# A graph network kernel: ACT's relu into a tile of its own, and six gather buffers in place of eight

## The chip, the cores and the metric

The kernel runs on one core of a Trainium2 chip. The time is the device time of one execution in microseconds (us); several executions are taken and their median is compared. The engines are PE (TensorE, matmuls; its weight loads are shown as PEld), DVE (VectorE), ACT (ScalarE), POOL (GpSimd) and SP (SyncE). Each works through its own instructions in their order and waits for the others by semaphores.

## What is computed

A graph has 6250 nodes with 128 features each and 100000 edges, sorted by their target node `dst`; targets are dense at the low node numbers. There are two GINE layers, which also read a row for each edge, and then two GIN layers, which don't. Cut to the sums over edges, and with the layer norms and the residual additions named only:

```
h = relu(layernorm(x))
for l in 0, 1:                                   # GINE
    msg = relu(h[src] + edge_attr)               # one row of 128 numbers for each edge
    agg = segment_sum(msg, dst)
    h = relu(relu(batchnorm((h + agg) @ W1[l] + b1[l])) @ W2[l] + b2[l])
x = x + h
h = relu(layernorm(x))
for l in 0, 1:                                   # GIN
    agg = segment_sum(h[src], dst)
    h = relu(((1 + eps) * h + agg) @ wa.T + ba) @ wb.T + bb
x = x + h                                        # the relu of GIN comes after its first layer only
```

## The kernel before

**Groups.** The edges are cut into 98 groups of 1024 (128 partitions x G = 8 edges; the last group is smaller). For each group of a GINE layer (the loop at L958) the program issues, in this order:

1. `load_rows` (L620): SP loads the group's edge rows, 512 KB, three groups ahead (`AHEAD`).
2. `gather` (L635): POOL issues eight indirect DMAs (L639), one for each of the 8 edges of a partition. Each brings 128 rows of 512 bytes from the node table in DRAM to the tile `g`, 128 x 1024 float32, 4 KB in each partition. `g` has eight buffers in the GINE layers and four in the GIN layers. A gather into a buffer waits until the last reader of the group that used it before is done.
3. `places` (L644): DVE makes the one-hot matrix `onehot` of the edges' target columns (L648), as wide as the group's span of nodes.
4. `Counter.count` (L734): beside the sums, the two GINE layers count how many edges lead from each node to each window of target nodes, which the GIN layers use for the first 70 groups' edges (their sums are then dense products, L1051). One or two units of 256 edges are counted in an iteration: DVE makes one-hots `lo_j` and `at_j` (L741, L744), PE multiplies them (L756) into a PSUM bank `pa`, and DVE adds the bank to the window `win` (L732, in `flush`), one unit later. ACT clears windows (L718) and SP stores them.
5. `sums` (L652): DVE adds the edge rows to `g` in place (L655), ACT applies relu to `g` in place (L656), PE multiplies `g` by `onehot` in 8 float32 terms (L660; 16 matmul instructions) into a PSUM bank `pe`. PE uses `g` as its weights.
6. `Columns.later` and `add` (L690 to L697): DVE adds `pe` of the group before this one (`BEHIND` = 1) to the columns of `acc` (L692).

Within an iteration, then, DVE has the order: one-hots, count one-hots and window additions, L655 of group s, L692 of group s-1. PE has the counts' matmuls and then L660 of group s. ACT has clears and then L656. The order is written out by hand for all five engines (`in_order`, L220); only semaphores delay an instruction.

Between the layers the nodes' own work runs in chunks of 512 nodes (`Steps`): batch norm and two products, and a table of the new features is written to DRAM, which the next layer's gathers read. In the second GINE layer, the first layer's own terms are made again chunk by chunk inside the loop (L972 to L977; ACT L842, PE L331, ACT L853). The GIN layers (loop at L1134) gather for the last 28 groups only, rows of 768 bytes (bf16 in three parts), and call `sums` without edge rows: there `g` goes to PE as gathered.

`general` (L1155) is a slow path for inputs whose targets are spread in another way. It isn't taken with these inputs.

Of the kernel before, what the change touches and what calls it, by code (L numbers as in the profile page):

```python
# [9 lines left out]
F32 = mybir.dt.float32  # L10
# [3 lines left out]
AF = mybir.ActivationFunctionType  # L14
# [3 lines left out]
P = 128  # L18
D = 128
# [3 lines left out]
G = 8  # L23

W = 152
# [3 lines left out]
BEHIND = 1  # L29
# [64 lines left out]
def gnn_kernel(ctx: ExitStack, tc: tile.TileContext, t: dict, out: bass.AP):  # L94
# [21 lines left out]
    nc = tc.nc  # L116
# [10 lines left out]
    NG = NGF + 1  # L127
# [32 lines left out]
    edge = gine_pools.enter_context(tc.tile_pool(name="edge", bufs=1))  # L160
# [3 lines left out]
    srcs = big.tile([P, NG * G], I32)  # L164
# [230 lines left out]
    for b in range(0, CODES, P):  # L395
        n = min(P, CODES + CODES % 2 - b)
# [238 lines left out]
    def gather(pool, table, n, idx, bufs):  # L635
        width, kind = (3 * D, BF16) if in_parts(table) else (D, F32)
        g = pool.tile([P, G, width], kind, name="g", bufs=bufs)
        for j in range(G):
            nc.gpsimd.indirect_dma_start(  # L639
                out=g[:n, j, :], out_offset=None, in_=table,  # L640
                in_offset=bass.IndirectOffsetOnAxis(ap=idx[:n, j : j + 1], axis=0))
        return g

    def places(pool, table, dl, w):  # L644

        onehot = pool.tile([P, G, W], BF16 if in_parts(table) else F32, name="onehot",
                           bufs=3)[:, :, :w]
        nc.vector.tensor_tensor(onehot, cols[:, None, :w].to_broadcast([P, G, w]),  # L648
                                dl[:, :, None].to_broadcast([P, G, w]), ALU.is_equal)
        return onehot  # L650

    def sums(g, n, onehot, rows):  # L652

        if rows is not None:
            nc.vector.tensor_add(g[:n], g[:n], rows[:n])  # L655
            nc.scalar.activation(g[:n], g[:n], AF.Relu)  # L656
        pe = bank_e()[:, : onehot.shape[-1]]
        terms = [(j, f) for j in range(G) for f in range(0, g.shape[-1], D)]
        for j, f in terms:
            nc.tensor.matmul(pe, g[:n, j, f : f + D], onehot[:n, j, :], start=(j, f) == terms[0],  # L660
                             stop=(j, f) == terms[-1])
        return pe
# [289 lines left out]
    for l in range(2):  # L952

        first_stages, end = batch_norm(l)
        steps, rest = Steps(first_stages), list(chunks())
        cs = Columns(brow)
        u, first_u, last_u = (0, 0, half) if l == 0 else (half, half, NU)
        for s in range(NG):  # L958
            n = P if s < NGF else RP
            for r in range(l * NG + s, min(l * NG + s + AHEAD + 1, 2 * NG)):  # L960
                if r not in rows:
                    rows[r] = load_rows(gine, r % NG, P if r % NG < NGF else RP, AHEAD + 2)
            g = gather(edge, tables[l], n, srcs[:, s * G : (s + 1) * G], 8)
            onehot = places(edge, tables[l], dloc[:, s, :], plan.group(s))
            while u < last_u and (cost[u] - cost[first_u]) * (NG - 6) < (s + 1) * (
                    cost[last_u] - cost[first_u]):
                counter.count(u)
                u += 1
                if u == NU:
                    counter.end()  # L970
            counter.some_chores()
            if own_later:  # L972

                got = None
                for stage in own_stages:
                    got = stage(*own_later[0], got)
                own_later.pop(0)  # L977
            cs.ready(max(s - BEHIND, 0))
            cs.later(s, sums(g, n, onehot, rows.pop(l * NG + s)), BEHIND)
            rows[l * NG + s] = None  # L980
            steps.step()
            ready = gine_ends[rest[0][2] + rest[0][3]]
            if ready is not None and ready <= s + 1 - BEHIND:
                steps.begin(rest.pop(0))
            if l == 0 and s == AHEAD:
                unplanned = nc.values_load(total[0:1, 0:1], min_val=0, max_val=1)
        if l:
            ahead[:] = chunks()
            load_ahead(x)
        while cs.late:  # L990
            cs.add(*cs.late.pop(0))
        for chunk in rest:
            steps.begin(chunk)
            steps.step()
        steps.end()
        if l == 0:
            own_stages = gine_nodes(0, *end())[:3]
            staged(*gine_rows(tables[1], own_stages[0]))
            own_later = list(chunks())
# [96 lines left out]
    for l in range(2):  # L1096
        stages = gin_nodes(l)
        if l == 0:
            def high_part(c, b0, n0, w, z):
                pt, xp = rows_of(bank_n, z, w), xps[1]  # L1100
                h = work.tile([P, CB, D], F32, name="h")
                for n, b in parts_of(w):
                    to = xp[:n, b0 + b.start : b0 + b.stop, :D]
                    nc.scalar.copy(to, pt[:n, b, :])
                    nc.vector.tensor_tensor(h[:n, b, :], pt[:n, b, :], to, ALU.subtract)
                return h

            stages = (*stages, high_part, parts_stages(xps[1], tables[3])[1])
        made, steps, rest, cs = products[l], Steps(stages), list(chunks()), Columns(brow)

        def pieces_to(n):
            while made.done < min(n, len(order)):
                made.piece()
                for _ in range(5):
                    if own_later:
                        _, b0, n0, w = own_later.pop(0)
                        of_parts(xps[0], b0, -(-w // P), own["eps1"], acc[:, n0 : n0 + w])

        def begin_nodes(s):


            u = made.counted()
            for chunk in rest:
                counted, gathered = (d[chunk[2] + chunk[3]] for d in (counted_ends, gine_ends))
                by_counts = counted is not None and u >= counted
                by_groups = gathered is not None and s >= gathered and (
                    u == NU or chunk[2] >= gathered_from)
                if by_counts or by_groups:
                    rest.remove(chunk)
                    steps.begin(chunk)  # L1130
                    return

        start = made.done
        for s in range(KG, NG):  # L1134
            n = P if s < NGF else RP
            g = gather(gin, tables[2 + l], n, srcs[:, s * G : (s + 1) * G], 4)
            onehot = places(gin, tables[2 + l], dloc[:, s, :], plan.group(s))
            pieces_to(start + max(3, -(-(s - KG + 1) * (len(order) - start) // (NG - KG - 1))))
            cs.ready(max(s - BEHIND, KG))
            cs.later(s, sums(g, n, onehot, None), BEHIND)  # L1140
            steps.step()
            begin_nodes(s + 1 - BEHIND)
        while cs.late:
            cs.add(*cs.late.pop(0))
        if l == 0:
            made.load()
        for chunk in rest:
            steps.begin(chunk)
            steps.step()
        steps.end()  # L1150
# [39 lines left out]
    def of_windows(pool, table, g, n, with_rows):  # L1190

        col = g * G
        idx = small.tile([P, G], I32, name="idx")
        dl = small.tile([P, G], F32, name="dl")
        if isinstance(g, int):
            nc.vector.tensor_copy(idx, srcs[:, col : col + G])
            nc.vector.tensor_scalar_add(dl, dloc[:, g, :], float(W))
            at_g = slice(g, g + 1)
        else:
            nc.vector.tensor_copy(idx, srcs[:, bass.ds(col, G)])  # L1200
            nc.vector.tensor_scalar_add(
                dl, dloc.rearrange("p g j -> p (g j)")[:, bass.ds(col, G)], float(W))
            at_g = bass.ds(g, 1)
        k = nc.values_load(wrow[0:1, at_g], min_val=1, max_val=NW)
        b = nc.values_load(brow[0:1, at_g], engines=[mybir.EngineType.DVE],
                           min_val=0, max_val=N)
        with tc.For_i(0, k) as i:
            nc.vector.tensor_scalar_add(dl, dl, -float(W))
            g_t = gather(pool, table, n, idx, 2)
            rows = load_rows(pool, g, n, 2) if with_rows else None  # L1210
            pe = sums(g_t, n, places(pool, table, dl, W), rows)
            at_c = nc.s_assert_within(b + i * W, min_val=0, max_val=N)
            a = acc[:, bass.ds(at_c, W)]
            nc.vector.tensor_add(a, a, pe)
# [29 lines left out]
```

## Time and profile before

| what | value |
|---|---|
| median of 10 runs | 3326.07 us (3320.42 to 3335.35) |
| the profiled execution, its own time | 3324.98 us |
| its span, first to last instruction | 3322.9 us |
| mean granted clock of TensorE | 0.73 |
| busy: PE, PEld, DVE, ACT, POOL | 1820.7, 1138.4, 1376.6, 454.8, 2039.5 us |
| gathers L639: count, mean | 2016, 985 ns |
| adds L655: count, mean | 196, 1219 ns |
| relus L656: count, mean | 196, 1056 ns |
| gathers of GINE layer 0: first start, last end | 41.5 us, 1217.0 us |
| gathers of GINE layer 1: first start, last end | 1276.7 us, 2412.5 us |
| gathers of the GIN layers | 2542.6 to 3276.2 us |

How to read the lines of the profile: `L639 POOL DMA_INDIRECT g<-table,srcs x2016 | 1986.7, 985 | 1086.7` means line 639 of the kernel, engine, operation, what it writes and reads, how many; then the busy time in us, the mean of one in ns, and the idle time of that engine just before these instructions, with what ended it. "issue" stands for no wait that the profile could tell, "remote" for a semaphore whose source it couldn't name. Lines of the time line begin with the start and the duration in us; the bracket at the end is the idle time before, and what ended it. PE's starts are recorded, its ends are modelled.

### The profile page before, as it was taken

The numbers are of one execution on the slowest core, as the hardware profiler recorded it, in microseconds if no ns is written. First come the engines' busy times: TensorE is split into PE (matmuls) and PEld (weight loads), VectorE is DVE, ScalarE is ACT, GpSimd is POOL, SyncE is SP. The second block draws the span as 40 slices with busy tenths as digits, with TensorE's granted clock in tenths as the row PEclk, the third lists the DMA queues.
The fourth block names the chain that finished last, engine by engine and source line by source line (L and its number), as shares of the span: only waits on it lengthen the run. The fifth ranks groups of instructions, "written<-read, shape, count | busy, mean of one in ns | idle before, by whom it ended". The sixth has DMA issues, their size and how long they took to land. (4 is left out here: it accounts for less than half of the span.)

```text
span 3322.9 us, 27768 instructions
## 1 busy us (share of the span) xinstructions
PE 1820.7 (55%) x8459; PEld 1138.4 (34%) x8460; DVE 1376.6 (41%) x3051; ACT 454.8 (14%) x579; POOL 2039.5 (61%) x2118
## 2 busy tenths in 40 slices
PE   1355445544444453355543454344557678858997
PEld 0233333333323342243432333222333334424443
DVE  5355455455555552244554455355552111111112
ACT  1200001010111112121110111111032001110000
POOL 6466666666676646666666666666614566546662
PEclk9999995556666676555555556666678888878998
DMA  3323242424243424233424344243447455545663
GB/s 117 113 89 91 89 127 89 129 88 130 86 134 95 124 84 135 69 96 121 135 90 121 93 133 133 85 128 100 151 119 231 147 171 169 184 136 185 222 218 122
DMA packets 259227, 421.87 MB, mean 127 GB/s; under 512 B 40864, under 2 KB 187088, under 8 KB 259068
## 3 DMA queue, kind: packets, MB, share of 16 engines
q1 hardware_dynamic: 173532, 184.05, 17.9%
q0 software_dynamic: 71424, 146.03, 14.7%
q10 hardware_dynamic: 14112, 89.92, 7.6%
q8 instruction: 69, 1.13, 0.1%
q14 instruction: 90, 0.74, 0.1%
HBM read 352.48 MB, written 67.36 MB: 126 GB/s over the span
## 5 line engine op out<-in xcount | busy, mean ns | idle before, releaser
L639 POOL DMA_INDIRECT g<-table,srcs x2016 | 1986.7, 985 | 1086.7 <-issue 900.4
L660 PE MATMUL pe<-onehot,g 128*128 128x16 f32 (+25 forms) x4480 | 745.4, 334 | 583.5 <-issue 241.8
L660 PEld LDWEIGHTS pe<-onehot,g 128*128 128x128 f32 x3136 | 610.1, 293 | 647.0 <-ACT g L656 301.8
L756 PE MATMUL pa<-at_j,lo_j 128*128 128x450 f16 (+22 forms) x1172 | 422.5, 498 | 649.3 <-DVE win L732 345.3
L1051 PE MATMUL pa<-piece,xp 128*128 128x512 f16 x2058 | 498.0, 395 | 66.5 <-issue 64.2
L732 DVE TENSOR_TENSOR win<-win,pa 128x450 f32 (+17 forms) x586 | 315.5, 575 | 408.8 <-remote 304.4
L756 PEld LDWEIGHTS <-lo_j 128*128 128x128 f16 x1172 | 157.7, 140 | 857.5 <-issue 466.1
L656 ACT ACTIVATE g<-g 128x1024 f32<-128x1024 f32 x196 | 207.0, 1056 | 1545.0 <-DVE g L655 817.3
L692 DVE TENSOR_TENSOR acc<-acc,pe 128x112 f32 (+18 forms) x252 | 61.1, 243 | 778.8 <-remote 328.3
L744 DVE TENSOR_SCALAR at_j<-numbers,code 128x1470 f16<-128x1470 f16 (+13 forms) x560 | 363.0, 648 | 0.0
L1051 PEld LDWEIGHTS <-xp 128*128 128x128 bf16 x2058 | 204.5, 100 | 352.2 <-issue 146.5
L655 DVE TENSOR_TENSOR g<-g,rows 128x1024 f32<-128x1024 f32 x196 | 238.8, 1219 | 23.9 <-DMA g<-table,srcs 20.1
L648 DVE TENSOR_TENSOR onehot<-numbers,dloc 128x896 bf16<-128x896 f32 (+23 forms) x252 | 224.4, 891 | 4.6 <-issue 4.6
L741 DVE TENSOR_SCALAR lo_j<-numbers,slo 128x128 f16<-128x128 f16 x560 | 153.5, 274 | 0.0
L660 PEld LDWEIGHTS <-g 128*128 128x128 bf16 (+1 forms) x1344 | 90.4, 105 | 78.7 <-issue 55.0
L801 DVE BATCH_NORM_STATS2 bst<-pn 128x6 f32<-128x512 f32 (+1 forms) x26 | 17.3, 666 | 213.7 <-remote 153.0
L718 ACT COPY win<-zero 128x1001 f32<-128x1001 f32 x98 | 92.9, 1019 | 74.3 <-remote 74.3
L692 DVE TENSOR_TENSOR acc<-acc,pa 128x256 f32 x28 | 11.8, 421 | 182.9 <-remote 116.7
L920 ACT ACTIVATE y<-pn,vcols 128x512 f32<-128x512 f32 (+1 forms) x26 | 17.1, 659 | 472.3 <-PE pn L331 421.2
L319 POOL TENSOR_SCALAR h<-xs,rs 128x128 f32<-128x128 f32 x49 | 21.4, 452 | 91.1 <-DVE rs L312 85.5
L828 DVE TENSOR_TENSOR xs<-xs,pn 128x512 f32<-128x512 f32 (+1 forms) x26 | 17.0, 654 | 78.9 <-PE pn L347 51.0
L802 ACT COPY acc<-pn 128x512 f32<-128x512 f32 (+1 forms) x26 | 14.6, 560 | 247.2 <-DVE bst L801 201.6
(162 smaller groups left out, 637.0 us busy)
## 6 DMA issues: line engine op xcount, KB each, us to landing
rows<-in_edge_attr SPq DMA_DIRECT2D x194, 512.0 KB
piece<-counts ACTq DMA_DIRECT2D x98, 896.0 KB
counts<-win SPq DMA_DIRECT2D x98, 448.0 KB
g<-table,srcs POOLq DMA_INDIRECT x2016
table<-xp SPq DMA_DIRECT2D x24, 384.0 KB
x_first<-in_x SPq DMA_DIRECT2D x8, 384.0 KB
table<-x_first SPq DMA_DIRECT2D x8, 384.0 KB
xs<-table SPq DMA_DIRECT2D x12, 256.0 KB
```

The costliest lines, as they stand in the source:

```text
L639: nc.gpsimd.indirect_dma_start(out=g[:n, j, :], out_offset=None, in_=table, in_offset=bass.IndirectOffsetOnAxis(ap=idx[:n, j : j + 1], axi ...
L648: nc.vector.tensor_tensor(onehot, cols[:, None, :w].to_broadcast([P, G, w]), dl[:, :, None].to_broadcast([P, G, w]), ALU.is_equal)
L655: nc.vector.tensor_add(g[:n], g[:n], rows[:n])
L656: nc.scalar.activation(g[:n], g[:n], AF.Relu)
L660: nc.tensor.matmul(pe, g[:n, j, f : f + D], onehot[:n, j, :], start=(j, f) == terms[0], stop=(j, f) == terms[-1])
L692: nc.vector.tensor_add(a, a, sums)
L718: self.chores.append(lambda v=flat[:, q * n : (q + 1) * n], n=n: nc.scalar.copy(v, self.zero.to_broadcast([P, n])))
L732: nc.vector.tensor_add(v, v, pa[:, : n * w].rearrange("p (b w) -> p b w", w=w))
L741: nc.vector.tensor_scalar(lo_j, cols16[:, MID : MID + P], slo[:, col : col + 1], None, op0=ALU.is_equal)
L744: nc.vector.tensor_scalar(at_j[:, :width], cols16[:, :width], code[:, col : col + 1], None, op0=ALU.is_equal)
L756: nc.tensor.matmul(pa[:, : n * w], los[j], ats[j][:, b * w : (b + n) * w], start=j == 0, stop=j == UT - 1)
L1051: nc.tensor.matmul(pa, xp[:, q * QB + b, i * D : (i + 1) * D], v[:, :, b, :], start=q + b + i == 0, stop=q == NQ - 1 and b == QB - 1 and i ...
```

## The change

`sums` takes one more argument, the pool. Where there are edge rows, it allocates a tile `m` of the same shape as `g`, with two buffers, ACT writes its relu into `m`, and PE's matmuls read `m`. The GINE loop's `gather` is called with six buffers. The calls for places without edge rows only pass a pool, and no `m` is made there.

```diff
-    def sums(g, n, onehot, rows):
+    def sums(g, n, onehot, rows, pool):
 
         if rows is not None:
             nc.vector.tensor_add(g[:n], g[:n], rows[:n])
-            nc.scalar.activation(g[:n], g[:n], AF.Relu)
+            m = pool.tile([P, G, D], F32, name="m", bufs=2)
+            nc.scalar.activation(m[:n], g[:n], AF.Relu)
+            g = m
         pe = bank_e()[:, : onehot.shape[-1]]
...
-            g = gather(edge, tables[l], n, srcs[:, s * G : (s + 1) * G], 8)
+            g = gather(edge, tables[l], n, srcs[:, s * G : (s + 1) * G], 6)
...
-            cs.later(s, sums(g, n, onehot, rows.pop(l * NG + s)), BEHIND)
+            cs.later(s, sums(g, n, onehot, rows.pop(l * NG + s), edge), BEHIND)
...
-            cs.later(s, sums(g, n, onehot, None), BEHIND)
+            cs.later(s, sums(g, n, onehot, None, gin), BEHIND)
...
-            pe = sums(g_t, n, places(pool, table, dl, W), rows)
+            pe = sums(g_t, n, places(pool, table, dl, W), rows, pool)
```

## The prediction

> **What bounds the kernel now.** I read the page first, then the waits, then the time line of each engine. The change touches the two layers with edge rows (GINE), 159.9 to 1217.0 and 1276.7 to 2412.5 us of the span. The page gives two of the steps in question:
>
> ```profile
> L639 POOL DMA_INDIRECT g<-table,srcs x2016 | 1986.7, 985 | 1086.7 <-issue 900.4
> ...
> L656 ACT ACTIVATE g<-g 128x1024 f32<-128x1024 f32 x196 | 207.0, 1056 | 1545.0 <-DVE g L655 817.3
> ```
>
> A group is eight gathers. They follow each other at 0.95 + 0.30 us, so a group takes POOL at least 10.0 us, and in layer 1 some 10.35 us, since a few gathers take 1.2 to 2.0 us. The adds L655, counted in the time line, come every 11.7 us in both layers. POOL alone doesn't explain 11.7, and DVE (busy 1376.6 us of the span) and ACT (454.8) even less. The list of waits names the rest:
>
> ```profile
> DVE acc L692 <- remote: 445.0, 33, 59.4
> ...
> DVE win L732 <- remote: 304.4, 38, 18.7
> ```
>
> DVE sits idle some 750 us before two instructions that read a result of PE in PSUM. What PE does then is plainest where its work is simple, at the start of the third layer. PE's time line, then POOL's:
>
> ```profile
> 2517.19 27.36 PE L1051 MATMUL pa<-piece,xp 128*128 128x512 f16 x126
> ...
> 2573.84 0.27 PE L790 MATMUL pe<-ident_b,xp 128*128 128x128 bf16 x1 [3.23 <-issue]
> 2575.94 0.27 PE L790 MATMUL pe<-ident_b,xp 128*128 128x128 bf16 x1 [1.83 <-issue]
> ...
> 2589.73 4.00 PE L790 MATMUL pe<-ident_b,xp 128*128 128x128 bf16 x36 [1.18 <-ACT acc L792]
> ```
>
> ```profile
> 2542.61 1.01 POOL L639 DMA_INDIRECT g<-table,srcs  x1 [17.56 <-DMA piece<-counts]
> ...
> 2581.53 0.95 POOL L639 DMA_INDIRECT g<-table,srcs  x1 [0.30 <-issue]
> ```
>
> While POOL rests, 126 matmuls take 27.36 us. POOL then gathers without a break from 2542.6 to 2582.5; some 15 us into that, PE falls to one small matmul every 1.4 to 3.5 us, and it recovers at 2585 to 2588, some 3 to 5 us after the last gather. One coincidence proves nothing, so here is an ordinary cycle of layer 0, from the time lines of POOL, of DVE and of ACT:
>
> ```profile
> 464.56 0.94 POOL L639 DMA_INDIRECT g<-table,srcs  x1 [0.30 <-issue]
> 468.82 0.94 POOL L639 DMA_INDIRECT g<-table,srcs  x1 [3.32 <-issue]
> ```
>
> ```profile
> 468.18 0.83 DVE L732 TENSOR_TENSOR win<-win,pa 128x300 f32 x2 [9.70 <-remote]
> ```
>
> ```profile
> 470.57 1.06 ACT L656 ACTIVATE g<-g 128x1024 f32<-128x1024 f32 x1 [14.76 <-DVE g L655]
> ```
>
> POOL gathers from 445.13 to 465.50, finds no free buffer and stops; 2.7 us later DVE, stuck for 9.70 us, gets PE's result, and 0.64 us after that POOL goes on. ACT's relu of the next group comes only later. And one of layer 1, in the same three views:
>
> ```profile
> 1816.43 0.95 POOL L639 DMA_INDIRECT g<-table,srcs  x1 [0.30 <-issue]
> 1822.00 0.95 POOL L639 DMA_INDIRECT g<-table,srcs  x1 [4.62 <-issue]
> ```
>
> ```profile
> 1821.30 0.22 DVE L692 TENSOR_TENSOR acc<-acc,pe 128x64 f32 x1 [16.00 <-remote]
> ```
>
> ```profile
> 1826.82 1.06 ACT L656 ACTIVATE g<-g 128x1024 f32<-128x1024 f32 x1 [20.38 <-DVE g L655]
> ```
>
> The stops are strikingly alike. Between groups, the time line of L639 has 39 of over 1 us in layer 0 after group 10 (128 us in all, mean 3.3) and 29 in layer 1 after its first run (123 us, mean 4.25), nearly all of 2 to 6 us. If PE's slow spells ended on their own, POOL would meet them at any phase and the stops would scatter widely. I read it so: **a long run of gathers holds PE's results back, and only POOL's stop lets them through.** POOL's time (10.0 to 10.35 us a group) plus its stops sets the 11.7. What carries the message inside the chip, no view here shows.
>
> The Trainium skill, "TensorE: Matmul & The Clock Gate", section "Seeing it yourself", has another cause for a slow PE: the clock gate, which it says has been seen stuck at a quarter for over 50 us, in events that aren't reliable. The row decides against it as far as the records go:
>
> ```profile
> 457.00:468.00 11.00, 3.99 (x18) 3.21 (x19) 1.48 (x5) 0.00 (x0) 6.62 (x7) 1.00 0.24 78
> ```
>
> Its granted clock is 1.00 in just the 11 us in which DVE waited. By that page the change would cost nothing (3326 us); by the row it costs the sum below.
>
> **The change, part by part.** *ACT's relu into m.* Same instruction, same 1.056 us; the nearest ACT row with two different tiles, L718, takes 1.019 us for 1001 elements, 1.042 scaled to 1024. Taken as nothing; bounds -0.01 and 0 us a group. *A wait on m.* It has two buffers, so relu of group s needs PE to be done with s-2. DVE's add of s stands behind L692 of s-2, which waits for just that, so ACT finds it done: 0. Were that cover gone, it would cost up to one group of matmuls (3.65 us) before relu, and win's clears L718 behind it. *PE's waits.* PE no longer waits for the gathers' landings, since it reads m; they had landed long before, and PE starts 0.05 us after relu's end (448.27 to 448.32): 0 to -10 us in all. *Memory.* Six buffers of g and two of m are what eight of g were. *Places without rows* (the GIN layers) make the same instructions as before.
>
> *The release of g.* Before, gather k waits for PE's matmuls of group k-8. After, it waits for ACT's relu of k-6. It is no matter of data coming late: the last gather of layer 1 ends at 2412.5 and its add comes at 2443.70; two groups less of lead (2 x 10.35 us) still leave 10 us. It is a matter of how long POOL stops. PE's result comes as before, about 3 us after the stop, but POOL then needs the add and the relu, too:
> - Layer 0: relu ends at 471.63, plus the 0.64 us to wake POOL, 472.27 in place of 468.82, so 3.45 us later; the cycle before (relu 447.21 + 1.06 + 0.63 against 445.13) gives 3.77. I take 3.6.
> - Layer 1: 1826.82 + 1.06 + 0.70 = 1828.58 in place of 1822.00: 6.6 us later, since DVE still has one-hots, counts and the add to do.
>
> In those extra microseconds POOL is quiet, PE runs freely and the consumers get ahead, so the next run of gathers is longer and there are fewer stops. Adds come 7.5 us apart in the fast stretches of layer 0 (445.91 to 453.45) and about 5.5 us apart in layer 1. Layer 0: 88 groups and 39 stops, 2.26 groups a stop. The next add needs a result that was held back at about 13 us after POOL's resumption; 3.6 us more let it through, so one more group: 3.26, 27 stops of 3.3 + 3.6 = 6.9 us, 186 in place of 128: **+58**. Layer 1: 89 groups, 29 stops, 3.07 a stop; 6.6/5.5 gives 1.2 more: 4.27, 20.8 stops of 10.85 us, 225 in place of 123: **+102**. Bounds: with no longer runs, 39 x 3.6 + 29 x 6.6 = +331; with two more groups a run, 20.7 x 6.9 - 128 = +15 and 17.6 x 10.85 - 123 = +68, together +83. I take the middle way because the gain in groups follows from the rows' own distances.
>
> At the start of layer 1 POOL gathers nine groups in one run (to 1368.2) while PE crawls; gather 106 then waits for a relu that came at 1380, so the run ends a group earlier: -10 us (bounds -10 and 0). Sum: 58 + 102 - 10 = **+150** on the span of 3322.9, 3473; the run lasts 2.1 us longer than its span, and the median 1.1 more than this run: **3476 us**.
>
> The Trainium skill, "Perfetto Trace Analysis", section "Identifying Performance Opportunities" (Optimization Strategy), says that a bubble which repeats on the engine that should be full can mean too few buffers. The stops above are such bubbles; as an estimate by that rule, 251 us x 8/6 would add 84 us, some 3410. It speaks against the change too, but doesn't see which event ends the bubble.
>
> **The rivals.** *Nothing moves.* PE's slow spells have a cause of their own (the float32 matmuls, the clock) and the gathers, landed dozens of us early, hide everything. For it: data are never late, and PEclk is 0.5 to 0.6 over most of layer 1. Against it: the slow spell at clock 1.00, and stops that are all alike. 3326 us; chance 0.17. *Faster: stops like those of GIN.* There POOL stops every group, near 2.2 us (3064.50 to 3067.69), and PE isn't starved. If in layer 0 the block comes one group earlier, before the results are held back, and ACT's message frees POOL without a crawl, each stop could shrink to 2.2 us: 39 x 1.1 + 29 x 2.05 = 102 less, 3224. It decides as soon as runs become shorter than some 13 us. Against it: consumers at 7.5 us a group outrun POOL at 10, so that POOL isn't blocked in time and the runs grow. Chance 0.13. *The change doesn't do what it says*: m keeps ACT waiting for PE after all, so that g hangs on PE with a lead of six: about 39 x 3.3 more stops' worth at worst, 3450. The order on DVE excludes it nearly: 0.02.
>
> **How the numbers follow.** Forecast 0.68, own range 3322.9 + 83 - 10 to 3322.9 + 331, with 3 us around it: 3399 to 3657. The measurement of this kernel tells about 0.2% (6.7 us) from no change. Slower: 0.68, the last rival, and 0.02 of the first: 0.72. Same: 0.13. Faster: 0.13 and the remaining 0.02 of the first: 0.15. The range must hold 0.8, so it takes in the first rival at its foot, and loses a little at the top: 3315 to 3620.
>
> **What would show it.** L656 becomes m<-g, still 1.06 us. POOL's stops in the GINE layers: about 27 and 21 in place of 39 and 29, some 7 and 11 us long, each ended by ACT's relu; runs of 3 and 4 to 5 groups. The adds come every 12.4 and 12.9 us. GIN keeps its length. It is wrong if the stops keep 3 to 4 us, or if DVE's long waits for PE go on after POOL has stopped; then PE is slow by itself.

## The result, and the profile after

| | before | after |
|---|---|---|
| median | 3324.46 us (31 runs) | 3497.41 us (9 runs, 3474.62 to 3513.14) |
| ratio | 1 | 1.0517, 95% interval 1.0500 to 1.0535 |
| span of the profiled execution | 3322.9 us | 3502.4 us |
| gathers of layer 0, first start to last end | 1175.5 us | 1286.5 us |
| gathers of layer 1 | 1135.9 us | 1220.8 us |

The change makes the kernel 5.2% slower. Two lines of `sums` are new, so the numbers move: the add is now L656, the relu L658, PE's matmuls L663, and `acc`, `win` and the counts L695, L735 and L759. The groups of the page for the gathers and the relu, with busy time, mean of one in ns, and idle time ahead of them:

```profile
L639 POOL DMA_INDIRECT g<-table,srcs x2016 | 1961.7, 973 | 1308.7 <-issue 625.9
...
L658 ACT ACTIVATE m<-g 128x1024 f32<-128x1024 f32 x196 | 207.0, 1056 | 1749.7 <-DVE g L656 786.6
```

The relu is the same 1056 ns, and the gathers are even a little shorter (973 in place of 985 ns). What grew is POOL's idle time, 1086.7 to 1308.7 us. The waits of the changed kernel (total us, times, longest) say whom POOL waits for:

```profile
DVE acc L695 <- remote: 625.8, 39, 60.3
...
POOL g L639 <- ACT m L658: 498.1, 60, 41.7
...
DVE win L735 <- remote: 376.8, 60, 20.1
```

Before, no such line of POOL's stood in the list; now 60 stops, 498.1 us, end with ACT's relu. DVE's two long waits for PE have grown with them, 445.0 to 625.8 us and 304.4 to 376.8 us. An ordinary cycle of layer 0, in the time lines of POOL, DVE and ACT (start, duration, and in brackets the idle time before and what ended it):

```profile
500.60 0.94 POOL L639 DMA_INDIRECT g<-table,srcs  x1 [0.30 <-issue]
508.07 0.94 POOL L639 DMA_INDIRECT g<-table,srcs  x1 [6.54 <-ACT m L658]
```

```profile
504.63 0.83 DVE L735 TENSOR_TENSOR win<-win,pa 128x300 f32 x2 [12.66 <-remote]
505.37 1.22 DVE L656 TENSOR_TENSOR g<-g,rows 128x1024 f32<-128x1024 f32 x1
```

```profile
506.75 1.06 ACT L658 ACTIVATE m<-g 128x1024 f32<-128x1024 f32 x1 [17.38 <-DVE g L656]
```

POOL stops at 501.54. PE's result reaches DVE at 504.63, 3.1 us after that, as it did before. Then, however, POOL waits on for the add (505.37), the relu (506.75 to 507.81) and 0.26 us more. In every stop over 1 us from group 6 on, the first gather now starts 0.3 us after the end of a relu; before, none of the stops of the steady part (from group 10 of layer 0, and all of layer 1) did; there POOL goes on within 1 us of a read by DVE that had waited for PE in 49 of 68.

The gaps over 1 us between POOL's groups, counted in the time line of L639, account for the time:

| stops | before | after | difference |
|---|---|---|---|
| layer 0, groups 1 to 9 | 2, 38.0 us | 3, 58.8 us | +20.8 |
| layer 0 from group 10 | 39, 127.9 us (mean 3.28) | 34, 236.0 us (mean 6.94) | +108.1 |
| layer 1 | 29, 123.2 us (mean 4.25) | 26, 216.8 us (mean 8.34) | +93.6 |

That is 222.5 us. The gathers' own busy time in the two layers gives back 24.0 (1560.8 to 1536.8), the small gaps between gathers 2.6, the stretch between the layers' gathers 11.6 (59.7 to 48.1) and the one after them 4.8 (910.4 to 905.6): with a lead of two groups less, fewer adds are outstanding when the last gather ends. The rest is 179.5 us, the difference of the spans.

### The profile page after: what moved, and what is told of

Its sections match the earlier page's. It is cut to its first block, busy times and chain, and to the rows that moved or that the text cites. A ratio compares the mean times of both kernels' runs of the same rounds, so it can differ in the third digit from the quotient of the medians.

```text
span 3502.4 us, 27611 instructions
## 1 busy us (share of the span) xinstructions
PE 1808.9 (52%) x8459; PEld 1130.2 (32%) x8460; DVE 1379.1 (39%) x3051; ACT 455.2 (13%) x579; POOL 2014.2 (58%) x2118
## 4 chain that ended last, share of the span: by engine, by line
another core or an unknown queue 31%; PE 24%; issue 16%; DVE 14%; POOL 7%; ACT 4%; DMA 3%; DVEq 2%; ACTq 1%; SPq 0%; POOLq 0%
PE pa L1054 11%; PE pe L663 8%; POOL g L639 6%; DVE at_j L747 4%; DVE win L735 3%; DVE g L656 2%; PE pa L759 2%; ACT m L658 2%; DMA g<-table,srcs 2%; DVE lo_j L744 2%; PE pn L331 1%; DVE onehot L648 1%; ACT win L721 1%; DVE acc L695 1%
## 5 line engine op out<-in xcount | busy, mean ns | idle before, releaser
L639 POOL DMA_INDIRECT g<-table,srcs x2016 | 1961.7, 973 | 1308.7 <-issue 625.9
L663 PE MATMUL pe<-onehot,m 128*128 128x24 f32 (+18 forms) x3136 | 635.5, 375 | 524.7 <-ACT m L658 321.4
L759 PE MATMUL pa<-at_j,lo_j 128*128 128x450 f16 (+22 forms) x1172 | 423.9, 500 | 820.7 <-DVE win L735 431.3
L663 PEld LDWEIGHTS pe<-onehot,m 128*128 128x128 f32 x3136 | 603.3, 291 | 640.7 <-ACT m L658 407.8
L735 DVE TENSOR_TENSOR win<-win,pa 128x450 f32 (+17 forms) x586 | 316.7, 575 | 496.6 <-remote 376.8
L759 PEld LDWEIGHTS <-lo_j 128*128 128x128 f16 x1172 | 158.2, 141 | 1029.2 <-issue 540.7
L658 ACT ACTIVATE m<-g 128x1024 f32<-128x1024 f32 x196 | 207.0, 1056 | 1749.7 <-DVE g L656 786.6
L695 DVE TENSOR_TENSOR acc<-acc,pe 128x112 f32 (+18 forms) x252 | 61.1, 242 | 920.7 <-remote 520.6
L656 DVE TENSOR_TENSOR g<-g,rows 128x1024 f32<-128x1024 f32 x196 | 238.9, 1219 | 20.4 <-DMA g<-table,srcs 17.2
L663 PE MATMUL pe<-onehot,g 128*128 128x136 bf16 (+6 forms) x1344 | 104.5, 233 | 59.6 <-issue 43.9
L663 PEld LDWEIGHTS <-g 128*128 128x128 bf16 (+1 forms) x1344 | 89.7, 104 | 85.8 <-issue 62.1
L695 DVE TENSOR_TENSOR acc<-acc,pa 128x256 f32 x28 | 11.8, 421 | 181.3 <-remote 105.2
L331 PE MATMUL pn<-acc,L_gnn_W 128*128 128x512 f32 (+1 forms) x52 | 35.4, 771 | 38.2 <-issue 27.3
```

The source lines that it names most:

```text
L639: nc.gpsimd.indirect_dma_start(out=g[:n, j, :], out_offset=None, in_=table, in_offset=bass.IndirectOffsetOnAxis(ap=idx[:n, j : j + 1], axi ...
L658: nc.scalar.activation(m[:n], g[:n], AF.Relu)
L695: nc.vector.tensor_add(a, a, sums)
L735: nc.vector.tensor_add(v, v, pa[:, : n * w].rearrange("p (b w) -> p b w", w=w))
L759: nc.tensor.matmul(pa[:, : n * w], los[j], ats[j][:, b * w : (b + n) * w], start=j == 0, stop=j == UT - 1)
```

## The experiments

The runs were made on several chips, and **the chips differ**. The kernel before takes 3285.57 and 3287.35 us on two of them (D and E), near the 3324.46 us of the first measurement, and 2811.58, 2805.96 and 2810.03 us on three others (A, B and C). Every ratio below is against the kernel before on the same chip.

**The kernel before on a chip of the second kind (C).**

> The kernel before itself, for its trace on the chip on which it takes 2806 to 2812 us. My theory: no stop of POOL in the steady part of the GINE layers, and none of the 0.3 to 1.3 us gaps that DVE's and PE's instructions show on the first chip while POOL gathers (DVE's 18 small tensor_scalars L515 at the start, 8.6 us there, take under 1.5 us; the transposes L790 of the third layer run through); the first gather of group 6 comes some 16 us earlier than with six buffers. Rival (PE runs behind there too, and the depth alone hides it): PE's gaps during gathers are there, and DVE's adds come 20 us or more behind the gathers.

2813.85 us. There POOL has no stop over 1 us in the two GINE layers, and once the head start is used up the adds follow the gathers' ends by 1.7 to 6.4 us, 1.8 in the median. The first chip's waits of the kernel before, and then chip C's:

```profile
PEld L756 <- issue: 466.1, 543, 19.2
DVE acc L692 <- remote: 445.0, 33, 59.4
```

```profile
PEld L756 <- issue: 102.6, 462, 1.9
```

The longest time that PE's weight loads L756 wait with no event that the profile shows falls from 19.2 to 1.9 us, and the waits "remote" are gone from the list of the longest. DVE shows the same at the start, in 18 tiny instructions at 56 to 76 us, when POOL already gathers: first chip, then chip C.

```profile
L515 DVE TENSOR_SCALAR diff_r<-lo_u x18: 130/131/142, 67.7 to 76.3; 1x1 f32<-1x1 f32 x18
...
  issue: 7.0, 7
```

```profile
L515 DVE TENSOR_SCALAR diff_r<-lo_u x18: 130/131/142, 56.1 to 57.1; 1x1 f32<-1x1 f32 x18
```

Each takes 131 ns on both; on the first chip there are 7.0 us of gaps before them (8.6 us from first to last, against 1.0). So the slow spells aren't the work of PE's float32 matmuls alone, and not of the gathers alone either: gathers of the same kind run on chip C for a whole layer without a break, and hold nobody back.

**The changed kernel there (B).**

> The changed kernel itself, unchanged. The first four runs were made on a chip on which the kernel before takes 2812 us, with no stop of POOL in the steady part and every add within 2 us of its gather's end. My theory (the cost is the length of POOL's stops): on such a chip there are no stops to lengthen, so the changed kernel is within 1.5% of the kernel before there (as the six buffers alone, +0.5%, and the relu into another tile alone, +1.1%, were); on a chip on which the kernel before takes some 3325 us it is again 5% slower. Rival (the wait for ACT's relu costs by itself, by making every group's gather later): 4% or more slower on any chip.

2817.38 us, ratio 1.0043 (1.0030 to 1.0056). Without stops in the steady part there is nothing to lengthen. What is left is one wait in the time line of POOL, 11.66 us before group 6, which needs the relu of group 0 while the preparations still run; the medians differ by 11.4 us:

```profile
101.11 0.94 POOL L639 DMA_INDIRECT g<-table,srcs  x1 [0.30 <-issue]
113.72 0.94 POOL L639 DMA_INDIRECT g<-table,srcs  x1 [11.66 <-ACT m L658]
```

**Six buffers alone (A).** One character of the kernel before.

```diff
-            g = gather(edge, tables[l], n, srcs[:, s * G : (s + 1) * G], 8)
+            g = gather(edge, tables[l], n, srcs[:, s * G : (s + 1) * G], 6)
```

> The kernel before with six gather buffers in place of eight and nothing else: ACT's relu still writes back into g, so a gather waits for PE's matmuls of group k-6. My theory (what costs is which event ends POOL's stop): the stops in the steady part keep some 3.3 and 4.2 us, runs keep 2.3 and 3.1 groups, only the first laps lose two groups of lead; 3315 to 3345 us. Rival (the number of buffers costs): most of the change's +173 us is here, over 3400 us, with stops of 6 us or more.

2825.28 us, ratio 1.0052 (1.0032 to 1.0071): one stop of 16.2 us before group 6. The theories were told apart by stops that this chip doesn't have, so the run leaves them open. It does show that there the earlier release by the relu is a gain, as one would naively read it: 16.2 us (ended by PE, here) become 11.7 (ended by the relu, on B).

**Five buffers alone (E).** The same edit with a 5, on a chip that has the stops.

> The kernel before with five gather buffers and nothing else: ACT's relu writes back into g, a gather waits for PE's matmuls of group k-5. On a chip with POOL's stops (the kernel before at 3280 to 3330 us there): my theory (the event that ends the stop costs, not the depth) expects steady stops of 3 to 4.5 us as with eight buffers, runs of 2.3 and 3.1 groups, and at most 30 us for the lead lost at the start, 0 to 1% slower; the rival (depth costs) expects more than the changed kernel's 5%, stops over 6 us. On a chip without stops (2806 to 2814 us) both expect one stop of some 26 us before group 5 and 0.7 to 1.1% slower.

3276.29 us, ratio 0.9964 (0.9948 to 0.9980): with three buffers less the kernel is not slower at all, even a little below the 0 to 1% expected. The stops from group 10 of layer 0 are 31 of 3.63 us, those of layer 1 31 of 3.87 us, about the length of the kernel before. **As long as PE's matmuls end the stops, going from eight to five buffers costs nothing; the 5% comes with the tile m**, that is, with the event that lets POOL go on. (The changed kernel itself wasn't run on D or E, nor m with eight buffers on any chip with the stops.) A stop of layer 1, in the time lines of POOL, DVE and ACT:

```profile
1881.29 0.94 POOL L639 DMA_INDIRECT g<-table,srcs  x1 [4.28 <-issue]
```

```profile
1880.59 0.24 DVE L692 TENSOR_TENSOR acc<-acc,pe 128x80 f32 x1 [6.95 <-PE pe L660]
```

```profile
1886.46 1.06 ACT L656 ACTIVATE g<-g 128x1024 f32<-128x1024 f32 x1 [11.68 <-DMA g<-table,srcs]
```

POOL goes on 0.70 us after DVE got PE's result, and 5.2 us before ACT's next relu. In 48 of the 62 steady stops it goes on within 1 us of such a read.

The Trainium skill, "Perfetto Trace Analysis", section "Identifying Performance Opportunities", reads bubbles that repeat on the engine that should be full as a possible lack of buffers. Here they repeat some 60 times and aren't that: five buffers in place of eight leave the time 0.4% lower.

**Two buffers with m (D).**

```diff
-            g = gather(edge, tables[l], n, srcs[:, s * G : (s + 1) * G], 6)
+            g = gather(edge, tables[l], n, srcs[:, s * G : (s + 1) * G], 2)
```

> The changed kernel with two gather buffers in place of six (m keeps two). My theory for the second chip (buffers buy only the head start that POOL takes while the preparations run, since the adds follow the gathers' ends by 2 us): one stop of POOL of some 52 us before group 2 (relu of group 0 ends near 113.5 us, POOL is there at 62 us), stops of under 1 us later, 2850 to 2890 us. Rival (the lead matters in the steady part): stops at most groups, over 2950 us.

3489.88 us, ratio 1.0621 (1.0587 to 1.0655), on a chip that has the stops, so the expected times don't apply. The stops are those of the changed kernel with six: 34 of 6.67 us from group 10 of layer 0, 31 of 7.66 us in layer 1. Four buffers less add about one point to the 5.2% of the other chip, and the start explains most of that: 83.7 us of stops before group 10 in place of 58.8. The same from the other side: with the relu as the event, depth hardly moves the stops.

At its start this run also has what the other runs lack: a long rest of POOL on a chip with the stops, while the other engines work. With two buffers POOL has nothing to gather from 61.5 to 123.75 us, while DVE, ACT and PE prepare the first groups; with seven (the next run, same chip D) it gathers on to 118.2 us, but for one stop of 6.85. The 18 tiny instructions of DVE, two buffers and then seven:

```profile
L515 DVE TENSOR_SCALAR diff_r<-lo_u x18: 130/131/142, 66.3 to 67.3; 1x1 f32<-1x1 f32 x18
```

```profile
L515 DVE TENSOR_SCALAR diff_r<-lo_u x18: 130/131/143, 64.0 to 71.7; 1x1 f32<-1x1 f32 x18
...
  issue: 6.0, 6
```

With POOL at rest they run through in 1.0 us, as on chip C; no engine's list of waits has an "issue" from 62 to 120 us, and the first relu ends at 123.5 us. With POOL gathering it ends at 147.9 us. On this chip, then, it is POOL's gathers that hold the other engines' starts back, at least in this stretch.

**Seven buffers and one of m (D).**

```diff
-            m = pool.tile([P, G, D], F32, name="m", bufs=2)
+            m = pool.tile([P, G, D], F32, name="m", bufs=1)
...
-            g = gather(edge, tables[l], n, srcs[:, s * G : (s + 1) * G], 6)
+            g = gather(edge, tables[l], n, srcs[:, s * G : (s + 1) * G], 7)
```

> The changed kernel with seven gather buffers and one of m, the same memory. My theory for the second chip (the +0.43% there are the 11.7 us that POOL waits before group 6): POOL gets to group 7 at 113.4 us, when the relu of group 0 has just ended, so nothing is left, within 0.2% of the kernel before. Rival (the tile m, or the wait for it, costs): 0.3% or more slower than before.

3393.93 us, ratio 1.0333 (1.0309 to 1.0357); the expected time was for a chip without stops, and the rival's 0.3% or more came true on this one. Its waits:

```profile
ACT m L658 <- remote: 576.1, 37, 31.2
...
DVE acc L695 <- remote: 493.5, 48, 59.2
```

With one m, the relu of group s waits for PE to be done with group s-1, and the add of s stands ahead of DVE's wait for that, so nothing covers it. The 576.1 us are all of ACT's idle time before those relus. Counted from the end of the add (or of ACT's own work, where that is later), 55 of the 196 relus start over 0.5 us late, 353.5 us in all; in the changed kernel none does (0.46 us at most). Yet it loses less than two buffers of m do: the stops are 32 of 6.02 us from group 10 of layer 0 and 27 of 5.54 us in layer 1, between those released by PE (3.3 and 4.2) and those released by a relu behind an add (6.9 and 8.3). In layer 1, 22 of the 27 end with a relu whose add was long done, so that PE's held-back result starts the relu and the relu frees POOL. In layer 0 only 3 of the 32 do; the others still have the add between. The order of the stops is the order of the times, though on different chips; why layer 0 keeps its adds late is not shown.

**Relu into the rows, and add into the rows (A).** Two ways to release g without m, at eight buffers: `activation(rows[:n], g[:n], AF.Relu)`, and `tensor_add(rows[:n], g[:n], rows[:n])` with the relu in place there; PE reads `rows`.

> Eight gather buffers as before, and ACT's relu writes into the tile of the edge rows, which PE then reads; no tile m. A gather waits for ACT's relu of group k-8, the event of the changed kernel at the old depth. My theory: the stops are those of the changed kernel, near 6.9 us in layer 0 and 8.5 us in layer 1, each ended by a relu; 3460 to 3510 us. Rival (the number of buffers costs): the old depth gives the old time, 3310 to 3345 us.

> Eight gather buffers; DVE's add writes into the tile of the edge rows, ACT's relu works there in place, PE reads it. A gather waits for DVE's add of group k-8, some 1.1 us ahead of the relu. My theory: stops some 1.1 us shorter than with the relu's release, 5.8 and 7.4 us; by the balance of the changed kernel's trace (about 13 us of free running after a stop, 7.5 and 5.5 us a group for the consumers) a group costs 0.34 and 0.4 us less than with the relu, so some 70 us less than the changed kernel, 3400 to 3455 us. Rival (the earlier the release, the better, PE being no part of it): below the kernel before, under 3320 us. Rival (nothing but depth counts): 3310 to 3345 us.

2842.01 us, ratio 1.0111 (1.0094 to 1.0129), and 2842.26 us, 1.0098 (1.0071 to 1.0125). Chip A has no stops, so the question wasn't answered, and POOL has none in either run. What they lose is in the gathers themselves: 133 and 137 of the two layers' 1568 take over 1.1 us, against 77 with six buffers alone on the same chip, and all of them together take 38 and 42 us more than there. In both, SP's loads of edge rows wait for PE; whether those loads are what the gathers meet was not tried.

**A pause of POOL after each group (A).** Eight memsets of 128 x 48 behind the eight gathers of the kernel before.

> The kernel before, with eight small memsets (128 x 48) on POOL after the eight gathers of each GINE group, so that POOL gathers nothing for a short time after every 10 us; nothing else moves. My theory (a long run of gathers holds PE's results back, and a quiet POOL lets them through): if the pause is long enough to let PE's results through, DVE's waits for PE of over 5 us vanish, and the adds come every 10.3 us plus the pause; with a pause of 1 us that is 11.3 us and some 3250 us. If the pause is too short to let anything through, its length is added to each group of a run and the stops stay: 3380 to 3500 us. Rival (PE is slow by itself, POOL's stops follow from it): DVE's long waits stay as they are, and POOL's pauses only take time out of its stops, 3326 us.

3277.19 us, ratio 1.1659 (1.1633 to 1.1684). There is nothing to let through on this chip, so all of it is cost: 2.4 us a group. The time line of POOL shows where:

```profile
1506.05 1.52 POOL L966 MEMSET quiet<- 128x48 f32 x8
1508.16 1.74 POOL L639 DMA_INDIRECT g<-table,srcs  x1 [0.59 <-issue]
1510.20 0.94 POOL L639 DMA_INDIRECT g<-table,srcs  x1 [0.30 <-issue]
```

1.52 us of memsets, 0.59 in place of 0.30 us of gap, and a first gather of 1.74 in place of 0.94 us (1.58 in the mean of all first gathers). Whether a pause would pay on a chip with stops stays open.

**No gathers at all (B).** `gather` loads rows that lie side by side, with one DMA of SP.

> The kernel before, with the GINE layers' gathers left out: SP loads 1024 rows of the node table that lie side by side into the same tile with one DMA, the same 512 KB a group, so the sums are those of other nodes; POOL does nothing in these layers. My theory (gathers on POOL hold PE's results back): on a chip with the stops, DVE's waits of over 5 us before L692 and L732 are gone, the adds come every 7.5 us or less, and the whole takes 2500 to 2700 us. Rival (PE is slow by itself there): the long waits stay, adds every 10 us or more, over 3000 us. On a chip without stops both expect the consumers' own pace, 2300 to 2650 us, since the gathers alone set 10.2 us a group there.

2300.8 us against 2805.96, ratio 0.8198 (0.8174 to 0.8221). The adds come every 7.56 us in layer 0 (groups 20 to 97) and every 6.79 us in layer 1 (median 6.1): the consumers' own pace, for which the prediction took 7.5 and 5.5 from short stretches. This kernel was not run on a chip with stops; what stands nearest to it is the start of the run with two buffers on D.

**More work for DVE (D).** The one-hots of the GINE layers written eight times, in the kernel before and in the changed one.

> The kernel before with the one-hots L648 of the GINE layers written eight times over instead of once, 7 x 0.9 us more for DVE in a group. This makes the consumers slower than POOL on the second chip, so that POOL runs out of buffers and stops at nearly every group, each stop ended by PE's matmuls of group k-8, while nothing holds PE back. Both theories: DVE sets the pace, 3450 to 3650 us; it is the base for the next run.

> The changed kernel with the same seven additional one-hots a group. POOL stops at nearly every group, each stop ended by ACT's relu of group k-6. My theory (the stops cost only where PE's results are held back while POOL gathers): within 0.5% of the kernel before with the same additional one-hots. Rival (a stop that is ended by the relu costs by itself, 3.6 and 6.6 us each): 100 us or more above it. Rival (an earlier release is a gain wherever POOL is stopped): 20 us or more below it.

3728.14 us (ratio 1.1347, 1.1315 to 1.1379) and 3817.48 us (1.1625, 1.1592 to 1.1658): the changed kernel is 89 us, 2.4%, slower with the same addition, and so neither within my 0.5% nor over the rival's 100 us. I had expected a chip without stops; D has them, and PE is held back here too (464.0 us of "issue" before the count's weight loads). So the run doesn't show what stops cost where nothing is held back. It shows the price halved where DVE sets more of the pace: the stops of layer 0 from group 10 and of layer 1 grow from 540.3 to 712.7 us, 172 us, while the times differ by 89.

## Why the prediction was right

It said 3476 us, in a range from 3315 to 3620, and the median is 3497.41. Direction and mechanism hold, on chips that have the stops. That the measurement fell on such a chip was luck as far as the prediction knew: on B the same change gives 0.4%.

**What bounds the kernel.** That long runs of gathers hold PE's results back, and that POOL's stop lets them through, fits what the changed kernel shows. PE's matmul starts a microsecond, counted from the traces of the first chip (and of chip E with five buffers) by the time since POOL began a run of gathers (what lies between two stops of over 1 us), in layer 1 from 120 us after its first gather:

```
                 0-5   5-10  10-15  15-20  20-30  30-60 us
before           1.69  3.27  3.39   2.22   1.66   0.66
after            3.91  3.43  2.82   2.30   1.54   0.35
five in place    1.70  3.40  3.46   2.22   1.35   0.79
```

Up to some 15 us PE goes at its pace, and then it starves. (Where PE's result ends the stop, before and with five, the first 5 us are slow as well: add and relu are still to come.) On chip C PE starts 2.1 matmuls a microsecond over the same part of layer 1, through 879 us of gathers without a break. A count of starts alone doesn't tell a PE that is held back from one that waits for work; the 62 us of rest on D do, for DVE above all: the same instructions on the same chip lose their gaps when POOL stops. But the prediction spoke of it as a thing that gathers do. The runs on A, B and C show that it is a thing that gathers do on some chips; on the others the first rival ("nothing moves") is right within 0.4%. One chip's profile couldn't have told that.

**The relu, the wait on m, PE's waits.** As said: 1056 ns, and each of the 196 relus starts within 0.46 us of the end of its add or of ACT's work before it, so none waits for PE to be done with m. The run with one m shows what an uncovered wait is: 353.5 us behind the adds.

**The release of g.** The predicted chain (PE's result some 3 us after the stop, add, relu, 0.6 us to wake POOL) is the cycle shown above, 6.54 us there and 6.94 in the mean, against 6.9 predicted for layer 0. What failed is the step after it, "so one more group": runs of 3.26 groups and 27 stops were predicted; there are 34 stops, and a run has 2.6 groups. The 3.6 us more of a stop buy 3.6/7.56 = 0.48 groups, not a whole one, since a group takes 7.56 us of the consumers' time. With 13 us of free running and 6.9 of stop, (13 + 6.9)/7.56 = 2.6. So layer 0 costs +108 us where the sum had +58. This is an estimate that fits one layer: with 6.79 us a group, the same sum gives 3.1 groups for layer 1, where the trace has 3.4.

In layer 1 two sizes were off and nearly cancel, which is luck. One cycle gave 6.6 us more a stop; the mean is 8.34 against 4.25, 4.1 more. And 26 stops remain, not 20.8. The sum had 225 us of stops, the trace has 216.8, and +93.6 stands beside +102 - 10. The -10 for the layer's start doesn't show by itself: the first run does end a group earlier, but group 10 begins 114.5 us into the layer, in place of 113.6 before the change.

One reading of the lines was off without a consequence: the 11.7 us are the spacing of the gathers' groups (11.74 and 11.66 us), while the adds, which catch up, come every 11.2 us from group 10 on. After the change the adds come every 12.2 us in both layers, where 12.4 and 12.9 were forecast.

**What the sum left out.** Layer 0's start, +20.8 us: POOL runs into group 6 while the first group's relu is far off (41.7 us). The prediction let the change begin with group 8, at 159.9 us, and looked at the start for layer 1 only. Against it stand 24.0 us of shorter gathers and 16.4 us of shorter stretches behind the two layers' gathers, which it left out, too. With the small gaps' 2.6 they come to -22 us in all, so the span was missed by 29 us (3473 against 3502.4) where layer 0's runs alone would have made it 50.

**The rivals.** "Faster" is excluded on both chips on which the changed kernel ran. "Too few buffers", the reading behind the estimate of 3410 us, falls with the five buffers.

## What to carry to other kernels

Releasing a buffer at an earlier instruction isn't an earlier release in time: look at which event ends the producer's stop in an ordinary cycle, and write down what stands in the queue between that event and the new one. Where the consumers get ahead only in the producer's stops and shortly after, the length of the stop is the price, and here the number of buffers hardly entered; try the depth alone before blaming it. And when a stop's cause isn't in the program, measure on a second chip.

## What the runs showed of the hardware

Chips differ by 17 to 18% on the kernel before: 2806 to 2812 us on A, B and C, 3286 to 3324 us on D, E and in the first measurement, each steady within 1%. The difference lies in how fast DVE and PE start instructions while POOL issues indirect DMAs: gaps up to 19.2 us against 1.9 us before the same weight loads. On D, 18 instructions of DVE take 7.7 us from first to last start beside gathers and 1.0 us while POOL rests. The gathers themselves take 0.94 us with 0.30 us between them in both, and the mean granted clock is nearly the same (0.73 in the first trace, 0.76 on C). What the chips differ in, no run here shows.
